# Expert rows added to the result in memory, in place of storing them and gathering them at the end

## The chip, the cores and the metric

The kernel runs on one core of one Trainium2 chip. The metric is the device time of one execution in microseconds (us), lower is better. The kernel before was timed in three runs: 1007.42, 1012.31 and 1018.16 us, median 1012.31.

## What is computed

The input x has 2048 rows (tokens) of 1024 numbers in float32, in eight sequences of 256. The reference does three things, here in its own words with what doesn't matter left out:

```python
y = einsum('bsi,boi->bso', x, cond_weight[itok])            # one of 8 matrices per sequence
gu = y @ shared_w_gate_up.T;  g, u = split(gu, 2)
shared = (silu(g) * u) @ shared_w_down.T                    # for every token
probs = softmax(y @ gate_w.T);  vals, idx = top_k(probs, 2) # 2 of 16 experts per token
combine = one_hot(idx) * (vals / sum(vals))
out_e = (silu(g_e) * u_e) @ w_down[e].T                     # inner width 256 per expert
out = x + shared + sum_e combine[:, e] * out_e
```

So each row of the result is the sum of four rows: x, the shared expert, and two chosen experts, the last two scaled by their weights.

## The kernel before, in words

Matrix products are made in float32 precision out of three products of a high and a low part. Every weight tile is loaded by SP into a staging buffer "st" (four of them), ScalarE writes its high part and VectorE its low part into "hl" (the function split, L83 to L86), and TensorE multiplies. load_w (L114) does this, and after each load it takes one piece of other work from the list "between" and queues it on VectorE behind that split.

The stages follow one another:

1. cond(0) to cond(7) (L238) make y for the eight sequences and write it to the memory tensor y_d. The rows come back through POOL (y_block, L385, tile "yr") and are transposed. In between run the stages a to d of Up (L445), which make the shared expert's inner values for the first half of the tokens (groups 0 and 1 of 512 rows). Up needs sums of weights; they are made once (sums_weights, L507) and kept in the memory tensor ss_d.
2. For each group of 512 tokens, route (L287) picks two experts per token and gives each pair a place in its expert's list. scatter (L371) writes token number and weight to that place of the table tab_d, by eight indirect DMAs per group from POOL.
3. Behind the last group, VectorE sorts the experts by their number of tokens (L1046 to L1060), so that the n-th expert in order has at most CAPS[n] rows (304 down to 256); one indirect DMA reads the table (entries, L882). Further VectorE instructions (L1061, L1062, L1075 to L1086) work out, for each token, at which row of os_d its two expert results will stand (s1i, s2i).
4. shared_down (L614) makes the shared expert's output for groups 0 and 1, adds x, and stores the sum to xs_d.
5. The expert loop (L1108 to L1126) runs 16 times. expert_rows (L906) gathers the expert's tokens by eight to ten indirect DMAs on POOL (tiles "yg" and "yl"); expert_yt transposes and splits them; expert_up (L832) and expert_out (L921) multiply. expert_down (L844) leaves 128 rows, already scaled by their weights, in a tile "o"; expert_down_last (L860) leaves the rows above 256 in "ol". The tag "o" has three buffers. SP stores the tiles to os_d (L925, L928), at rows that the order of the experts fixes.
6. Up runs again for groups 2 and 3, without storing sums. Meanwhile combine (L778), on POOL, reads xs_d for group 0, adds the two expert rows of each token by two indirect DMAs per 128 tokens that accumulate in SBUF, and stores to out; then it does the same for group 2 with x as the base, and leaves the tiles in SBUF.
7. DownPair.run (L700) makes the shared output of groups 2 and 3 together. Ahead of it, combine runs for group 1 (with a store) and then for group 3. run adds its products to the tiles of groups 2 and 3 (add, L716 to L719) and stores them (L721 to L725). The buffers for groups 1 and 3 are those of the pool pd (L1167), which opens when X is no longer read.

A loop for experts that exceed their capacity (L1225 to L1230) stands at the end; with these inputs its body doesn't run.

The order in which each engine issues its instructions is fixed when the program is built: the framework's scheduler orders the instructions of each engine by their place in the program and by when a timeline of its own says they can start, and issue_after holds a piece of work behind a given instruction. Each engine, and each engine's DMA issuing, then runs its list in order, so an instruction that waits holds up what is behind it in the same list. Semaphore waits are put in from the reads and writes of tiles and memory tensors.

Of the kernel before, what the change touches and what calls it, by code (L numbers as in the profile page):

```python
# [8 lines left out]

F32 = mybir.dt.float32  # L10
FR = mybir.dt.float32r
BF = mybir.dt.bfloat16
I32 = mybir.dt.int32
# [20 lines left out]
ROW0 = [sum(CAPS[:n]) for n in range(E + 1)]  # L34
ZROW = ROW0[E]
PAD = 4 * T


@with_exitstack
def adapter_moe_kernel(ctx: ExitStack, tc: tile.TileContext, xT, x, itok, wc, gate, wgu, wd, sgu, sd, out):  # L40
# [20 lines left out]
    lpad.tile([P, 48], F32, tag="lpad", name="lpad")  # L61
# [6 lines left out]
    tab_d = dram.tile([E * SLOTS, 2], I32, tag="tab_d", name="tab_d")  # L68
    os_d = dram.tile([ZROW + 16, H], F32, tag="os_d", name="os_d")
    xs_d = dram.tile([T, H], F32, tag="xs_d", name="xs_d")  # L70
# [70 lines left out]
    gpk = cpool.tile([P, NC * 2 * E + P + 80], FR, tag="gpk", name="gpk")  # L141
# [13 lines left out]
    tid = [cpool.tile([P, T // P, 2], I32, tag=f"tid{r}", name=f"tid{r}") for r in range(2)]  # L155
    rev = cpool.tile([P, NB, E], F32, tag="rev", name="rev")
    caps = cpool.tile([P, E], F32, tag="caps", name="caps")
    row0 = cpool.tile([P, E], F32, tag="row0", name="row0")
    oneh = [cpool.tile([P, T // P, E], BF, tag=f"oneh{r}", name=f"oneh{r}") for r in range(2)]
    ranks = [cpool.tile([P, T // P], F32, tag=f"ranks{r}", name=f"ranks{r}") for r in range(2)]  # L160
    places = [cpool.tile([P, T // P], I32, tag=f"places{r}", name=f"places{r}") for r in range(2)]
    s1i = cpool.tile([P, T // P], I32, tag="s1i", name="s1i")
    s2i = cpool.tile([P, T // P], I32, tag="s2i", name="s2i")
# [4 lines left out]
    cw = cpool.tile([P, 3, E], F32, tag="cw", name="cw")  # L168
    ix = cpool.tile([P, E, 10], I32, tag="ix", name="ix")

    def constants(ring):
# [10 lines left out]
        rt = ring.tile([P, 1024], I32, tag="op", name="rt")  # L182
        revi = rt[:, : NB * E].rearrange("p (k e) -> p k e", k=NB)
# [4 lines left out]
        for j in range(E):  # L188
            nc.gpsimd.memset(row0[:, j : j + 1], float(ROW0[j] - ZROW))
# [5 lines left out]
    def tables(ring):  # L195
        gst = ring.tile([P, 1024], F32, tag="op", name="gst")
        gv = gst[:, : NC * E].rearrange("p (c e) -> p c e", c=NC)
        nc.sync.dma_start(gv, gate)
        gs = gpk[:, : NC * 2 * E].rearrange("p (c l e) -> p l c e", c=NC, l=2)
        split(gs[:, 0], gs[:, 1], gv)  # L200
        ti = ring.tile([P, 1024], I32, tag="op", name="ti")
        tw = ti[:, : 2 * E * SLOTS // P].rearrange("p (f o) -> p f o", o=2)
        nc.gpsimd.memset(tw[:, :, 0], PAD)
        nc.gpsimd.memset(tw[:, :, 1], 0)
        nc.sync.dma_start(tab_d.rearrange("(p f) o -> p f o", p=P), tw)


    def zeros(ys):
# [4 lines left out]
        nc.gpsimd.dma_start(os_d[ZROW : ZROW + 16, :], zr[:16, :])  # L213
# [73 lines left out]
    def route(g, lp):  # L287
# [71 lines left out]
        for r in range(2):  # L359
            rank = ranks[r][:, gs]  # L360
            sl = t2(f"sl{r}")
            v.tensor_copy(oneh[r][:, gs, :], oh[r])
# [8 lines left out]
    def scatter(g):  # L371
        for r in range(2):
# [11 lines left out]

    def y_block(tb, ys):  # L385
        r = ys.tile([P, 1024], F32, tag="yr", name="yr")

        nc.gpsimd.dma_start(r, y_d[tb].rearrange("a (i t) f -> (a i) (t f)", t=4))  # L388
# [15 lines left out]
    lps = {}  # L404

# [372 lines left out]
    def combine(pool, tbs, base):  # L778
        acc = [pool.tile([P, 1024], F32, tag="ca", name="ca") for tb in tbs]
        for a, tb in zip(acc, tbs):  # L780
            nc.gpsimd.dma_start(a, base[tb * P : (tb + 1) * P, :])
        for si in (s1i, s2i):
            for a, tb in zip(acc, tbs):
                nc.gpsimd.indirect_dma_start(
                    out=a,
                    out_offset=None,
                    in_=os_d[:, :],
                    in_offset=bass.IndirectOffsetOnAxis(ap=si[:, tb : tb + 1], axis=0),
                    compute_op=ALU.add,
                )  # L790
        return acc
# [90 lines left out]
    def entries(pool, column):  # L882
        cr = pool.tile([P, ENTRIES, 2], F32, tag="cr", name="cr", bufs=1)
# [10 lines left out]
        def weights():  # L894
            ct = psm.tile([P, 3, E], F32, tag="sm", name="ct")
            with tc.issue_after(last_product[0]):
                for j in range(3):
                    m = min(P, CAP - j * P)
                    nc.tensor.transpose(ct[:m, j, :], cr[:E, j * P : j * P + m, 1], ident[:E, :E])
            for j in range(3):  # L900
                m = min(P, CAP - j * P)
                nc.vector.tensor_copy(cw[:m, j, :], ct[:m, j, :])
# [18 lines left out]
    def expert_out(po, n, at):  # L921
        w = load_wd(expert_id(n))
        r0 = ROW0[n]
        for j in range(2):
            nc.sync.dma_start(os_d[r0 + j * P : r0 + (j + 1) * P, :], expert_down(po, at, w, j * P, cw[:, j, n : n + 1]))  # L925
        if CAPS[n] > MAIN:
            m = CAPS[n] - MAIN
            nc.sync.dma_start(os_d[r0 + MAIN : r0 + CAPS[n], :], expert_down_last(po, at3[n % 2], w, m, cw[:m, 2, n : n + 1]))  # L928
# [28 lines left out]
    between[:] = [None, after_loads(lambda: tables(ring))]  # L957
    cond(1, ys, early)
    between[:] = [turned(0, 0), None, both(turned(0, 1), fetch_rows(1, up.place(0, 1)))]
# [18 lines left out]
    scatter(0)  # L978
# [19 lines left out]
    scatter(1)  # L998
# [9 lines left out]
    fetch_rows(6, tv)()  # L1008
    h0, h1 = half_works(3, 0, tv), half_works(3, 1, tv)
    up.stage_c(0)  # L1010
    scatter(2)
    up.stage_c(1)
    between[:] = [turned(6, 0), None, turned(6, 1), None, h0[0], h0[1]]
    cond(7, ys)
    fetch_rows(7, tv)()
    up.stage_c(2)
    up.stage_c(3)
    between[:] = [turned(7, 0), turned(7, 1)]
    up.stage_d(0)
    between[:] = [h1[0], h1[1]]  # L1020
    up.stage_d(1)
# [239 lines left out]
```

## Time and profile before

| what | us |
|---|---|
| median of the three runs | 1012.31 |
| the profiled execution, its own time | 1013.59 |
| its span, first to last instruction | 1011.8 |
| TensorE (PE) busy | 980.6 |
| VectorE (DVE) busy | 684.5 |
| ScalarE (ACT) busy | 542.8 |
| POOL busy | 329.4 |
| the expert stage, roughly | 457 to 757 |

A second table gives the DMA issues that the change touches, as the profile lists them: how many, how large, and the median time from issue to landing.

| issue | queue | number | KB each | us to landing |
|---|---|---|---|---|
| os_d from o | SP | 32 | 512 | 3.9 |
| os_d from ol | SP | 11 | 32 to 192 | 4.1 to 5.7 |
| xs_d from acc | SP | 16 | 256 | 4.8 |
| ca from xs_d | POOL | 8 | 512 | 6.0 |
| ca from x | POOL | 8 | 512 | 6.3 |
| ca from os_d (s1i), accumulating | POOL | 16 | not listed | 9.3 |
| ca from os_d (s2i), accumulating | POOL | 16 | not listed | 13.4 |
| out from ca | POOL | 8 | 512 | 11.0 |
| yg from y_d, a quarter of a block | POOL | 128 | not listed | 5.3 |
| tab_d from tid | POOL | 32 | not listed | 5.1 |

How to read it: a name such as "ca<-os_d,s1i" means that the tile ca is written from the tensor os_d with the indices s1i. "L719" is a line of the kernel. PE is TensorE's matmuls; PEld its weight loads, which overlap them. Matmuls are pipelined, so the length of a single row (395 ns for a 512-wide one) isn't the rate; the rate is the time of a long unbroken stretch over its number of matmuls. A busy time of POOL for a DMA is the time to issue it. The DMA share is the mean busy share of the core's 16 DMA engines.

### The profile page before, as it was taken

The page shows a single profiled execution, that of the slowest core. Times are in us where ns is not written, and L with a number is a line of the kernel's source. Part 1 is how long each engine was busy: PE and PEld are TensorE (multiplying, and loading weights), DVE is VectorE, ACT ScalarE, POOL GpSimd, SP SyncE. Part 2 cuts the span into 40 slices and gives each one's busy share as a digit, 9 for nine tenths or more (in the row PEclk, how much of TensorE's full clock was granted, in tenths as well). Part 3 has the DMA queues.
Part 4 walks back from the last instruction along what each step waited for, and adds up shares of the span by engine and source line. Part 5 has one row for each costly group of instructions (what it writes and reads, how often), then busy time and mean ns, then how long its engine had stood idle before and what let it go on. Part 6 is the DMA issues. An engine that isn't in the chain of part 4 may idle for free.

```text
span 1011.8 us, 14020 instructions
## 1 busy us (share of the span) xinstructions
PE 980.6 (97%) x5004; PEld 835.8 (83%) x5004; DVE 684.5 (68%) x915; ACT 542.8 (54%) x729; POOL 329.4 (33%) x330
## 2 busy tenths in 40 slices
PE   8999999989999999999999999999999997999976
PEld 6888887768878888889999999999988886888855
DVE  4576878846855986639788788779693433678634
ACT  5555545645734642316677677677574644335430
POOL 2000250221040036607888856530004350003450
PEclk9999999999999999999999999999999998999998
DMA  8999968878678546858798887888878998425996
GB/s 274 315 320 360 336 191 294 322 205 293 174 206 266 208 91 203 279 176 276 250 320 297 307 291 276 291 301 287 287 259 275 284 325 230 123 86 158 270 269 180
DMA packets 84204, 256.93 MB, mean 254 GB/s; under 512 B 13084, under 2 KB 21420, under 8 KB 84124
## 3 DMA queue, kind: packets, MB, share of 16 engines
q1 hardware_dynamic: 51084, 176.58, 52.3%
q0 software_dynamic: 21904, 69.79, 23.2%
q10 hardware_dynamic: 11136, 9.57, 2.8%
q8 instruction: 41, 0.67, 0.3%
q14 instruction: 39, 0.32, 0.1%
HBM read 207.62 MB, written 48.28 MB: 253 GB/s over the span
## 4 chain that ended last, share of the span: by engine, by line
PE 67%; DMA 10%; DVE 3%; issue 2%; ACT 1%; POOL 0%; ACTq 0%; POOLq 0%; DVEq 0%
PE acc L497 23%; PE acc L134 13%; PE acc L136 13%; PE acc L135 13%; DMA ca<-os_d,s2i 2%; PE acc L867 2%; DMA st<-ss_d 2%; PE acc L691 2%; DMA raw<-sd 2%; DMA out<-ca 1%; DVE hl L85 1%; DMA ca<-os_d,s1i 1%; DVE op L85 1%; DMA st<-wc 1%; DMA y_d<-yrow 1%
## 5 line engine op out<-in xcount | busy, mean ns | idle before, releaser
L85 DVE TENSOR_TENSOR hl<-st,hl 128x1024 fp32r<-128x1024 f32 (+1 forms) x254 | 304.3, 1209 | 184.7 <-ACT hl L84 183.4
L84 ACT CAST hl<-st 128x1024 fp32r<-128x1024 f32 (+1 forms) x254 | 263.0, 1043 | 191.9 <-PE acc L136 96.9
L497 PE MATMUL acc<-op,hl 128*128 128x512 f32 x1296 | 304.3, 395 | 9.8 <-DVE op L85 5.6
L497 PEld LDWEIGHTS acc<-op,hl 128*128 128x128 f32 x1296 | 246.4, 191 | 62.7 <-DVE op L85 6.0
L799 POOL DMA_INDIRECT yg<-y_d,ix x128 | 172.9, 1351 | 95.2 <-DVE tt L218 47.6
L136 PE MATMUL acc<-yte,hl 128*128 128x256 f32 (+6 forms) x512 | 147.3, 288 | 0.0
L134 PE MATMUL acc<-yte,hl 128*128 128x256 f32 (+6 forms) x512 | 147.1, 288 | 0.0
L135 PE MATMUL acc<-yte,hl 128*128 128x256 f32 (+6 forms) x512 | 147.0, 287 | 0.0
L135 PE MATMUL acc<-hl 128*128 128x512 f32 x256 | 101.1, 395 | 1.2 <-DVE hl L85 1.1
L136 PE MATMUL acc<-hl 128*128 128x512 f32 x256 | 100.5, 392 | 0.0
L135 PEld LDWEIGHTS acc<-yte,hl 128*128 128x128 f32 x512 | 96.5, 188 | 0.6
L134 PEld LDWEIGHTS acc<-yte,hl 128*128 128x128 f32 x512 | 96.3, 188 | 0.6
L136 PEld LDWEIGHTS acc<-yte,hl 128*128 128x128 f32 x512 | 96.2, 188 | 0.0
L134 PE MATMUL acc<-hl 128*128 128x512 f32 x256 | 90.5, 392 | 3.2 <-ACT hl L84 3.2
L388 POOL DMA_DIRECT2D yr<-y_d x24 | 13.2, 550 | 224.4 <-DMA y_d<-yrow 107.5
L374 POOL DMA_INDIRECT tab_d<-tid,places x32 | 41.0, 1280 | 63.6 <-DVE ranks L364 46.3
L134 PEld LDWEIGHTS acc<-hl 128*128 128x128 f32 x256 | 48.0, 189 | 14.4 <-ACT hl L84 4.6
L135 PEld LDWEIGHTS acc<-hl 128*128 128x128 f32 x256 | 48.3, 189 | 13.3 <-DVE hl L85 3.1
L136 PEld LDWEIGHTS acc<-hl 128*128 128x128 f32 x256 | 48.5, 189 | 10.0
L691 PE MATMUL acc<-shl,op 128*128 128x512 f32 x192 | 45.8, 400 | 9.0 <-DVE ca L719 9.0
L691 PEld LDWEIGHTS acc<-shl,op 128*128 128x128 f32 x192 | 37.2, 194 | 17.3 <-DVE ca L719 9.4
L134 PE MATMUL acc<-hl,at 128*128 128x512 f32 x128 | 50.0, 391 | 0.0
(221 smaller groups left out, 1397.0 us busy)
## 6 DMA issues: line engine op xcount, KB each, us to landing
st<-wgu SPq DMA_DIRECT2D x64, 512.0 KB, 4.8
st<-wc SPq DMA_DIRECT2D x63, 512.0 KB, 6.0
st<-wd SPq DMA_DIRECT2D x32, 512.0 KB, 5.6
os_d<-o SPq DMA_DIRECT2D x32, 512.0 KB, 3.9
st<-ss_d SPq DMA_DIRECT2D x30, 512.0 KB, 8.1
st<-sd SPq DMA_DIRECT2D x30, 512.0 KB, 3.8
yr<-y_d POOLq DMA_DIRECT2D x24, 512.0 KB, 6.0
st<-sgu SPq DMA_DIRECT2D x24, 512.0 KB, 6.3
```

Source lines behind the costliest of these rows:

```text
L84: last_cast[0] = nc.scalar.copy(hi, src).ins
L85: last_split[0] = nc.vector.tensor_tensor(lo, src, hi.bitcast(F32), op=ALU.subtract).ins
L134: nc.tensor.matmul(ps, lhs[0], rhs[0], start=first, stop=False)
L135: nc.tensor.matmul(ps, lhs[0], rhs[1], start=False, stop=False)
L136: last_product[0] = nc.tensor.matmul(ps, lhs[1], rhs[0], start=False, stop=last).ins
L374: i = nc.gpsimd.indirect_dma_start(out=tab_d[:, :], out_offset=bass.IndirectOffsetOnAxis(ap=places[r][:, tb : tb + 1], axis=0), in_=tid[r] ...
L388: nc.gpsimd.dma_start(r, y_d[tb].rearrange("a (i t) f -> (a i) (t f)", t=4))
L497: last_product[0] = nc.tensor.matmul(ps, lhs[x], rhs[y], start=(first and c == 0 and i == 0), stop=(c == 3 and i == 2), skip_group_check=T ...
L691: nc.tensor.matmul(ps[k], lhs[x], rhs[y], start=(first and t == c == i == 0), stop=(t == c == 1 and i == 2), skip_group_check=True,)
L799: last_gather[0] = nc.gpsimd.indirect_dma_start(out=r[:, t * 256 : (t + 1) * 256], out_offset=None, in_=y_d.rearrange("k a p f -> (k a p) f"),
L867: nc.tensor.matmul(ps, a3[:, fi, :], w[fi][:, l, hs], start=(fi == 0 and l == 0), stop=(fi == 1 and l == 1))
```

## The change

- The result tensor out gets 320 more rows (ENTRIES) behind its 2048; they are cut off after the run. os_d, xs_d, the indices s1i and s2i, and the VectorE work for them are gone.
- A table entry has three numbers in place of two: the third is the token's row in out. Unused entries point at distinct spare rows. entries transposes two columns in place of one (six small transposes on TensorE in place of three) and leaves the row numbers in ctok.
- expert_out calls add_out for each of its two or three tiles: an indirect DMA from POOL that adds the rows to out in memory. The adds of one expert carry no dependency among themselves; each has a real wait for all adds of the expert before.
- shared_down writes to out in place of xs_d for groups 0 and 1. For groups 2 and 3, x_to_out copies x to out, 2 MB each, memory to memory, on SP behind stage d.
- combine is gone: groups 0 and 1 need nothing more, and for groups 2 and 3 added_rows loads out into SBUF, four plain loads of 512 KB each, behind all adds.
- The table's scatters of groups 0 and 1 move from stages a and b to behind cond(6), that of group 2 from stage c(0) to behind cond(7), that of group 3 from before to behind the last stage d, each behind the last y load; the filling of the table, and pieces of the "between" lists (row transposes, router products and choices, the weight sums t1 and t2 of DownPair) move to later loads.

```diff
-        for j in range(2):
-            nc.sync.dma_start(os_d[r0 + j * P : r0 + (j + 1) * P, :], expert_down(po, at, w, j * P, cw[:, j, n : n + 1]))
+        for j in range(2):
+            add_out(expert_down(po, at, w, j * P, cw[:, j, n : n + 1]), ctok[:, j, n : n + 1])
         if CAPS[n] > MAIN:
             m = CAPS[n] - MAIN
-            nc.sync.dma_start(os_d[r0 + MAIN : r0 + CAPS[n], :], expert_down_last(po, at3[n % 2], w, m, cw[:m, 2, n : n + 1]))
+            add_out(expert_down_last(po, at3[n % 2], w, m, cw[:m, 2, n : n + 1]), ctok[:m, 2, n : n + 1])
+        adds[:] = [adds[1], []]
...
+    adds = [[], []]
+
+    def add_out(o, tok):
+        i = nc.gpsimd.indirect_dma_start(
+            out=out, out_offset=bass.IndirectOffsetOnAxis(ap=tok, axis=0), in_=o, in_offset=None, compute_op=ALU.add
+        ).ins
+        for k in adds[0]:
+            tc.add_manual_dep(i, k.name, SYNC, reason="adds to the same rows")
+        for k in adds[1]:
+            tc.declare_no_dep(i, k, reason="different rows")
+        adds[1].append(i)
...
+    def x_to_out(k):
+        ts = slice(T // 2 + k * GT, T // 2 + (k + 1) * GT)
+        after_loads(lambda: nc.sync.dma_start(out[ts, :], x[ts, :]))()
...
     def scatter(g):
+        with tc.issue_after(last_rows[0]):
+            scatter_now(g)
...
-    between[:] = [None, after_loads(lambda: tables(ring))]
     cond(1, ys, early)
-    between[:] = [turned(0, 0), None, both(turned(0, 1), fetch_rows(1, up.place(0, 1)))]
+    between[:] = [turned(0, 0), None, both(turned(0, 1), fetch_rows(1, up.place(0, 1))), after_loads(lambda: tables(ring))]
...
     fetch_rows(6, tv)()
+    scatter(0)
+    scatter(1)
     h0, h1 = half_works(3, 0, tv), half_works(3, 1, tv)
     up.stage_c(0)
-    scatter(2)
     up.stage_c(1)
-    between[:] = [turned(6, 0), None, turned(6, 1), None, h0[0], h0[1]]
+    between[:] = [None, None, turned(6, 0), None, turned(6, 1), None, h0[0], h0[1]]
     cond(7, ys)
     fetch_rows(7, tv)()
+    scatter(2)
     up.stage_c(2)
     up.stage_c(3)
-    between[:] = [turned(7, 0), turned(7, 1)]
+    between[:] = [None, turned(7, 0)]
     up.stage_d(0)
-    between[:] = [h1[0], h1[1]]
+    x_to_out(0)
+    between[:] = [turned(7, 1), h1[0]]
     up.stage_d(1)
+    x_to_out(1)
+    between[:] = [h1[1]]
+    up.stage_d(2)
     between[:] = [choices(3)]
-    up.stage_d(2)
+    up.stage_d(3)
     scatter(3)
-    up.stage_d(3)
...
-    shared_down(0, G, ring, acc, xs_d)
+    shared_down(0, G, ring, acc, out)
...
-    combine_kept(pc, 0, xs_d)
...
-    store_kept()
-    acc2 = combine(pc[1], range(2 * NB, 3 * NB), x)
+    acc2 = added_rows(pc, 2)
     down = DownPair((G, S_), raw)
     up.stage_c(0)
     down.fetch()
-    for u in range(1, 4):
-        between[:] = down.work((down.t1, down.t2, lambda t: None)[u - 1])[:1]
-        up.stage_c(u)
-        held(down.work((down.t1, down.t2, lambda t: None)[u - 1])[1])
+    up.stage_c(1)
+    up.stage_c(2)
+    w1, w2 = down.work(down.t1), down.work(down.t2)
+    between[:] = w1[:1]
+    up.stage_c(3)
+    held(w1[1])
+    between[:] = [None, w2[0]]
     up.stage_d(0)
-    between[:] = [None] * 4 + down.work(down.s3)
+    between[:] = [None, w2[1], None, None] + down.work(down.s3)
...
     pd = pool("pd", 4)
-    combine_kept(pd, 1, xs_d)
-    store_kept()
-    acc3 = combine(pd[1], range(3 * NB, 4 * NB), x)
+    acc3 = added_rows(pd, 3)
     down.run(2, ring, (acc2, acc3), out)
```

## The prediction

> **What bounds the kernel now.** I read the page first, for the engine that is never idle.
>
> ```profile
> span 1011.8 us, 14020 instructions
> PE 980.6 (97%) x5004; PEld 835.8 (83%) x5004; DVE 684.5 (68%) x915; ACT 542.8 (54%) x729; POOL 329.4 (33%) x330
> PE   8999999989999999999999999999999997999976
> POOL 2000250221040036607888856530004350003450
> DMA  8999968878678546858798887888878998425996
> ```
>
> TensorE bounds nearly everything. Only the windows show where it falls short. Columns: window, us, busy time and instructions of each engine, clock, DMA share, GB/s.
>
> ```profile
> 470.00:550.00 80.00, 80.00 (x515) 74.90 (x515) 65.80 (x91) 58.94 (x95) 66.90 (x44) 1.00 0.86 290
> 832.00:853.00 21.00, 15.79 (x70) 12.76 (x68) 5.46 (x5) 11.73 (x16) 4.16 (x3) 0.99 0.97 262
> 853.00:890.00 37.00, 36.65 (x150) 30.09 (x151) 24.37 (x28) 9.49 (x10) 0.00 (x0) 0.92 0.40 122
> 970.00:990.00 20.00, 10.98 (x46) 8.81 (x45) 4.98 (x6) 3.06 (x3) 11.23 (x8) 0.80 1.04 210
> 978.00:987.00 9.00, 1.66 (x8) 1.04 (x6) 0.00 (x0) 0.00 (x0) 5.72 (x4) 0.73 1.06 200
> 990.00:1012.00 22.00, 15.75 (x62) 11.88 (x61) 8.75 (x14) 0.00 (x0) 0.00 (x0) 0.89 0.52 173
> ```
>
> There are two holes behind the experts. The DMA share is at or above 0.97 as each begins, and the clock is low after them. The timeline of TensorE and the chain of waits say what each waits for.
>
> ```profile
> 879.76 38.24 PE L497 MATMUL acc<-op,hl 128*128 128x512 f32 x168
> 988.68 5.61 PE L691 MATMUL acc<-shl,op 128*128 128x512 f32 x16 [9.02 <-DVE ca L719]
> ```
>
> ```profile
> 834.30 16.53 DMA raw<-sd
> ...
> 947.89 13.94 DMA out<-ca
> 961.83 0.28 issue
> 962.12 6.27 DMA ca<-x
> 968.39 0.26 issue
> 968.65 8.64 DMA ca<-os_d,s1i
> 977.30 0.26 issue
> 977.56 9.68 DMA ca<-os_d,s2i
> ```
>
> The undisturbed rate is 38.24 / 168 = 0.2276 us per 512-wide matmul. The last hole is the combine: the second half's buffers open only at 924, and base, two accumulating gathers, stores, then base and two gathers again follow one another until VectorE can add (L719) and give TensorE banks. The first hole is a weight load of 16.5 us beside the other combine; VectorE waits for it (L669).
>
> **What the Trainium skill says.** "DMA: Bandwidth & Descriptors", section Rules for kernel authors: an accumulate reads its destination and writes it later, so another access of the same bytes must wait for its semaphore. The trace agrees: the second gather starts at 977.56, after the first has landed. Same page, section Issuing engines are not separate DMA queues: SP, ACT and POOL share the same 16 engines, so moving stores from SP to POOL buys no bandwidth; no row here contradicts it. "Perfetto Trace Analysis", section DMA Instruction — SWDGE (GPSIMD): a POOL row ends when its descriptors are written, not when the data lands. The trace agrees: a combine gather is 1.54 us on POOL and lands after a median of 9.3. "SBUF — State Buffer", section Who interferes with whom: VectorE can hold up GpSimd's descriptor writing through shared ports. The expert gathers do stretch, from 0.95 to 5.18 us; no row names the cause.
>
> **The change, part by part.** The sum is made against the profiled execution, 1013.6 us (span 1011.8), 1.3 above the median of 1012.3.
>
> *The combine at the tail.* 970 to 1005.86 holds 46 + 62 = 108 matmuls, which at 0.2276 need 24.6 us; they took 35.9. Lost: 11.3 us. After the change acc3 needs only four plain loads of 512 KB behind 924 (like ca<-x, 6 us each, overlapping), ready by about 935, and its first use is behind 960. All 11.3 come back; next late is TensorE itself. Between 0 and -11.3; I take -11.
>
> *The combine at 768 to 850.* 832 to 890 holds 220 matmuls, 50.1 us in 58: 8 lost. Sixteen accumulating gathers, their bases and stores leave the DMA engines around this stage and the tail, and the weight sums (t1, t2) move one stage later, so VectorE no longer waits in front of a load. Between 0 and -8; I take -7.
>
> *The stores become adds.* 43 stores leave SP and 43 adds come onto POOL: 32 of 128 rows, 11 with 256 rows between them. SP then no longer holds weight loads behind a wait for ScalarE (40.2 us in all at L925); TensorE is full in this stage, so that gains nothing. Three resources pay.
>
> POOL: from 458.82 to 583.27, 71 gathers ran with no gap but 0.3 us each, 1.753 us apart. An add isn't in the trace; the nearest rows are the combine gathers, 1.54 us at least and 1.75 on the mean. Lower bound per add 1.84 with the gap, upper 2.6 (the longest row); I take 2.05. An expert with a third block then costs 9 x 1.753 + 3 x 2.05 = 21.9 us of POOL, where TensorE turns an expert over in 19.4. Before, POOL rested:
>
> ```profile
> 599.62 1.81 POOL L799 DMA_INDIRECT yg<-y_d,ix  x1 [0.30 <-issue]
> 606.59 0.95 POOL L799 DMA_INDIRECT yl<-y_d,ix  x1 [5.17 <-DVE tt L218]
> 664.39 0.95 POOL L799 DMA_INDIRECT yg<-y_d,ix  x1 [7.88 <-DVE tt L218]
> ```
>
> So POOL falls behind by 2.5 us per expert over 11 experts. What hides it: gathers run three to four experts ahead (those of expert 15 start at 664, while expert 11 is multiplied), so 50 us of lag is harmless if it is the gathers that lag. If the adds lag it is not: "o" has three buffers, an add must land before ScalarE writes the same buffer one expert later, and a third block is ready at 575.0 (expert 4) and its buffer wanted at 588.0. With 1.6 us of issue and some 5 to 7 us to land, slack is 5 to 6 us.
>
> DMA engines: hardware-queue transfers took 52.3% of 1011.8 us for 176.58 MB, 3.0 us per MB, 1.57 per 512 KB. In 978 to 987, nearly all accumulating gathers, 9 x 1.06 us moved 1.8 MB: 5.3 us per MB, 2.8 per block. The adds cost (2.8 - 1.57) x 34 blocks = 42 us more over 470 to 757, whose shares of 0.86, 0.85, 0.85 and 0.80 are 242 us; 284 of 287 would be used. It fits, barely, and full shares have left TensorE at full rate (757 to 832: share 0.98, 333 matmuls in 75 us, 0.225 each).
>
> The wait: the first add of an expert waits on POOL for all adds of the one before, with gathers queued behind it. The last was issued some 11 us earlier; I expect 0 to 2 us, inside the gathers' lead.
>
> Together, between -1 and +40 us; with adds ahead of gathers I take +3, for a few late weights.
>
> *The front.* Table scatters move behind later y loads, and the last table is ready about one stage (48 x 0.2276 = 10.9 us) later. First gathers then start near 396 instead of 384.8; the first expert's product starts near 457, so the cover holds; without it up to 10 us. The x copies (two of 2 MB, memory to memory) pass through SP's ring ahead of weight loads: at 3.0 us per MB 6 us each, beside a DMA share of 0.46 (350 to 390) and four weight buffers of 5.5 us each. Removed VectorE work (the index sums, about 8 us near 380 to 399) was under full TensorE. Three more transposes of 0.15 us: +0.5. TensorE idled 7.9 us in 150 to 300, of which a freer POOL may return 2. Between -4 and +10; I take -1 in all.
>
> Sum: 1013.6 - 11 - 7 + 3 - 1 = 997.6, near 997 against the median shown.
>
> **Rivals.** *Adds late in POOL's order* (30%). The order of a queue is fixed when the program is built; if it counts gathers as quicker than 1.75 us, adds stand behind gathers that POOL has not reached. By the end of expert 4 POOL has 67 gathers and 15 adds behind it, 458.8 + 117.5 + 30.8 = 607; the last add was ready at 575. Less the slack (6) and what TensorE has in hand (about 5), it loses some 20 at worst, half of that if gathers run at the 1.5 us of after 583. So +8 to +20 in place of +3: 1002 to 1016, likeliest 1008. For it: POOL without rest from 458 to 582 already. Against: an add comes earlier in the program than the gathers it competes with. A tail that gives back only one hole ends here too.
>
> *Adds dear in the DMA engines* (23%, slower). The known accumulates write to SBUF; these read and write memory rows. With c us per block the stage needs 242 + 34 (c - 1.57), and at the highest share seen, 1.05, there are 301. The 18 us gained are gone from c = 3.9. At 4.5 the stage takes 325 instead of 287, +38: 1033. For it: HBM carries the destination twice. Against: 809 to 820 moved 421 GB/s at share 1.03, so memory isn't the limit at 290.
>
> *The changed kernel runs as meant* (47%): 990 to 1003, likeliest 997.
>
> **How the numbers follow.** 1% is about what these runs (1007 to 1018) tell from no change. The first case lies on the faster side but for 1 in 100, the second in the middle but for 2 on either side, the third on the slower: 0.48, 0.27, 0.25. The range 988 to 1020 leaves out most of the third case and little else.
>
> **What would show it.** Right: no TensorE gap before L719 behind 970 and none for raw<-sd; shares of 0.95 to 1.0 in the experts; landing of adds below 10 us; expert period still 19.4. The first rival shows as ScalarE waiting for an add before "o" or "ol" with POOL busy throughout and periods near 21; the second as landings of 15 us and more with TensorE waiting for st. A TensorE gap at the table's transposes would make my front term wrong.

## The result, and the profile after

The changed kernel takes 1070.05 us (median of 4 runs, 1067.57 to 1073.65), the kernel before 1012.67 in the runs beside it: a ratio of 1.057, 95% interval 1.050 to 1.063. It is slower by some 57 us, where the forecast was 997 us with a range of 988 to 1020.

The profiled execution took 1068.68 us with a span of 1066.9. The page, with the same rows as shown of before:

```profile
span 1066.9 us, 13949 instructions
PE 1000.8 (94%) x5007; PEld 847.7 (79%) x5007; DVE 677.3 (63%) x891; ACT 541.5 (51%) x729; POOL 349.6 (33%) x313
PE   8999999999999989999988888798989599999997
POOL 2000201010434158178877777776222100000000
DMA  8899969686796557687678878778988733533322
```

TensorE now has 8s and a 7 in slices 21 to 26, where POOL has its 7s and 8s (19 to 27), and a 5 in slice 32. The last seven slices are better than before. The windows (columns: window, us, busy time and instructions of PE, PEld, DVE, ACT and POOL, clock, DMA share, GB/s) show the experts, first in the kernel before and then in the changed one, and the changed kernel from 839.69 us to its last product:

```profile
550.00:600.00 50.00, 50.00 (x345) 47.43 (x345) 38.67 (x51) 35.35 (x55) 37.55 (x30) 1.00 0.87 292
600.00:650.00 50.00, 50.00 (x329) 46.17 (x328) 40.91 (x53) 37.56 (x59) 27.27 (x22) 1.00 0.83 285
```

```profile
550.00:600.00 50.00, 44.30 (x256) 39.15 (x256) 30.25 (x41) 28.63 (x46) 37.37 (x25) 0.90 0.80 223
600.00:650.00 50.00, 41.42 (x256) 36.75 (x256) 30.03 (x41) 28.36 (x46) 37.38 (x25) 0.96 0.78 220
839.69:1061.00 221.31, 221.31 (x966) 182.74 (x966) 125.59 (x132) 99.45 (x132) 4.16 (x8) 0.99 0.38 124
```

In the experts there are 256 matmuls in 50 us, where the kernel before had 345 and 329, and the DMA engines are *less* busy than before. The last row is the second half behind its first 42 products: TensorE is full throughout, so neither of the two holes of the kernel before is left. (The experts end some 60 us later now, so the same work stands that much later on the clock.)

To see where the time went I cut the span at three marks that both kernels have: the first product of a third block, the rows of an expert above 256, which experts 0 to 10 have (expert 0, L867 before and L873 after), the last of them (expert 10), and the first product of the second half's Up (L497 before, L506 after).

| piece of the span, us | before | after | difference |
|---|---|---|---|
| start to the first third-block product | 488.4 | 485.6 | -2.8 |
| experts 0 to 10 ("the stretch") | 195.1 | 242.1 | +47.0 |
| experts 11 to 15, to the second half's first product ("the end of the experts") | 73.5 | 90.6 | +17.1 |
| the second half | 254.8 | 248.6 | -6.2 |
| span | 1011.8 | 1066.9 | +55.1 |

An expert of the stretch takes 24.2 us in place of 19.5. Three lines of the view of waits of the changed kernel within the stretch (who waits, for whom; us, times, longest) name ScalarE (ACT) waiting for adds to land, and GpSimd (POOL) waiting too:

```profile
ACT ol L874 <- DMA out<-ol,ctok: 41.9, 9, 5.9
ACT o L862 <- DMA out<-o,ctok: 30.9, 9, 7.4
POOL out L790 <- ACT ol L874: 23.4, 8, 3.8
```

And this is one expert of GpSimd's timeline (start, duration, what, in brackets the idle time before it), six of the eight gathers in the middle left out:

```profile
568.35 1.40 POOL L790 DMA_INDIRECT out<-ol,ctok  x1 [0.30 <-issue]
572.76 1.59 POOL L790 DMA_INDIRECT out<-o,ctok  x1 [3.02 <-ACT ol L874]
574.66 4.71 POOL L805 DMA_INDIRECT yl<-y_d,ix  x1 [0.30 <-DVE tt L218]
579.67 1.75 POOL L790 DMA_INDIRECT out<-o,ctok  x1 [0.30 <-ACT s L831]
581.73 1.01 POOL L805 DMA_INDIRECT yg<-y_d,ix  x1 [0.30 <-issue]
...
592.02 0.94 POOL L805 DMA_INDIRECT yg<-y_d,ix  x1 [0.30 <-issue]
593.26 1.39 POOL L790 DMA_INDIRECT out<-ol,ctok  x1 [0.30 <-issue]
597.56 1.59 POOL L790 DMA_INDIRECT out<-o,ctok  x1 [2.90 <-ACT ol L874]
```

The add of a third block (out<-ol) stands in the order behind eight gathers for an expert six places later. Once it is issued, the next expert's first add has to wait until it has landed, since both may touch the same rows; that wait is 2.9 us on the mean and 3.8 at most. The view puts it down to ScalarE's copy into ol, but that copy waits for the same landing (the first line above); run B2 below takes away only the wait of one expert's adds for those of the expert before, and GpSimd's gap is gone. In between there is no gap but 0.30. So GpSimd is either issuing or waiting for a landing, for 24.9 us in this expert, and TensorE follows it.

The piece behind the stretch shows a second thing. TensorE stops once more at the second half's first stage:

```profile
818.34 9.68 PE L506 MATMUL acc<-op,hl 128*128 128x512 f32 x42
839.69 2.93 PE L506 MATMUL acc<-op,hl 128*128 128x512 f32 x6 [11.66 <-ACT X L543]
```

```profile
827.00 1.53 POOL out L790
828.53 0.30 issue
828.84 10.11 DMA out<-o,ctok
839.05 0.59 ACT X L543
```

The second fence is the chain of waits: the tile X lies where source tiles of adds had been, so ScalarE's first copy into it (L543) waits until the last expert's last add has landed.

### The profile page after: what moved, and what is told of

Read it like the earlier page. It is cut to its first block, busy times and chain, and to the rows that moved or that the text cites. A ratio compares the mean times of both kernels' runs of the same rounds, so it can differ in the third digit from the quotient of the medians.

```text
span 1066.9 us, 13949 instructions
## 1 busy us (share of the span) xinstructions
PE 1000.8 (94%) x5007; PEld 847.7 (79%) x5007; DVE 677.3 (63%) x891; ACT 541.5 (51%) x729; POOL 349.6 (33%) x313
## 5 line engine op out<-in xcount | busy, mean ns | idle before, releaser
L506 PE MATMUL acc<-op,hl 128*128 128x512 f32 x1296 | 300.5, 392 | 11.8 <-ACT X L543 11.7
L506 PEld LDWEIGHTS acc<-op,hl 128*128 128x128 f32 x1296 | 243.9, 189 | 63.6 <-ACT X L543 12.3
L805 POOL DMA_INDIRECT yg<-y_d,ix x128 | 160.8, 1256 | 69.2 <-issue 40.3
L133 PE MATMUL acc<-yte,hl 128*128 128x256 f32 (+6 forms) x512 | 150.8, 296 | 14.9 <-DVE s L832 7.6
L135 PE MATMUL acc<-yte,hl 128*128 128x256 f32 (+6 forms) x512 | 149.9, 293 | 0.0
L134 PE MATMUL acc<-yte,hl 128*128 128x256 f32 (+6 forms) x512 | 149.7, 293 | 0.0
L133 PEld LDWEIGHTS acc<-yte,hl 128*128 128x128 f32 x512 | 99.1, 194 | 18.0 <-DVE s L832 9.4
L134 PEld LDWEIGHTS acc<-yte,hl 128*128 128x128 f32 x512 | 99.2, 194 | 0.4
L135 PEld LDWEIGHTS acc<-yte,hl 128*128 128x128 f32 x512 | 99.0, 194 | 0.0
L790 POOL DMA_INDIRECT out<-o,ctok x32 | 61.4, 1918 | 67.7 <-ACT ol L874 27.8
L134 PE MATMUL acc<-hl,at 128*128 128x512 f32 x128 | 56.2, 439 | 14.5 <-DVE hl L84 14.5
L133 PE MATMUL acc<-hl,at 128*128 128x512 f32 x128 | 55.2, 431 | 10.5 <-ACT hl L83 9.0
L862 ACT ACTIVATE o<-acc,cw 128x512 f32<-128x512 f32 x64 | 40.5, 684 | 38.5 <-DMA out<-o,ctok 37.9
```

The costliest lines, as they stand in the source:

```text
L133: nc.tensor.matmul(ps, lhs[0], rhs[0], start=first, stop=False)
L134: nc.tensor.matmul(ps, lhs[0], rhs[1], start=False, stop=False)
L135: last_product[0] = nc.tensor.matmul(ps, lhs[1], rhs[0], start=False, stop=last).ins
L506: last_product[0] = nc.tensor.matmul(ps, lhs[x], rhs[y], start=(first and c == 0 and i == 0), stop=(c == 3 and i == 2), skip_group_check=T ...
L790: i = nc.gpsimd.indirect_dma_start(out=out, out_offset=bass.IndirectOffsetOnAxis(ap=tok, axis=0), in_=o, in_offset=None, compute_op=ALU.ad ...
L805: last_gather[0] = nc.gpsimd.indirect_dma_start(out=r[:, t * 256 : (t + 1) * 256], out_offset=None, in_=y_d.rearrange("k a p f -> (k a p) f"),
```

## Experiments

Each run is one edit to a kernel, or several that are named, with its cut into the same four pieces. Two kernels with nearly the same order of GpSimd gave 210.4 and 222.4 us for the stretch, so less than some 12 us between two stretches decides nothing here. The kernel before took 1004 to 1034 us beside these runs, which were made on several chips (1014 to 1034 on one of them alone). Where no median is given, a whole time is that of one execution. So the argument rests on the pieces, compared with those of the profile above, and not on the whole times. The expectations count the end of the experts to the 43rd product of the second half, behind X's wait (112 us in the changed kernel); the table counts to the first (90.6).

| run | start | stretch | end of the experts | second half | whole |
|---|---|---|---|---|---|
| changed kernel | 485.6 | 242.1 | 90.6 | 248.6 | 1068.7 |
| A1 gathers of m behind adds of m-6 | 482.4 | 217.7 | 94.7 | 249.4 | 1046.4 |
| A2 behind adds of m-5 | 486.1 | 210.4 | 93.7 | 248.7 | 1040.7 |
| A3 behind adds of m-4 | 493.7 | 225.6 | 91.8 | 246.7 | 1059.6 |
| B1 plain scatters | 483.2 | 224.9 | 90.8 | 241.3 | 1042.0 |
| B2 two targets | 504.1 | 222.4 | 96.5 | 244.2 | 1069.0 |
| C before, no gathers of the combination | 486.6 | 195.1 | 79.7 | 235.3 | 998.9 |
| D1 rows loaded by SyncE | 485.2 | 236.0 | 84.5 | 244.6 | 1052.1 |
| D2 = A3 + D1 | 484.4 | 229.9 | 95.3 | 245.9 | 1057.3 (median 1047.0) |
| D3 = A2 + D1, X moved | 484.5 | 222.4 | 88.0 | 234.5 | 1031.2 |
| D4 = D3, finer order | 485.9 | 219.9 | 86.7 | 234.6 | 1028.4 |
| E1 = A1, half the bytes per add | 485.6 | 220.6 | 89.5 | 245.7 | 1041.0 |
| E2 = D4, half the bytes per add | 479.2 | 219.2 | 82.9 | 234.5 | 1018.0 |
| F1 = A1 without subtractions | 485.5 | 195.1 | 79.3 | 245.5 | 1007.2 |
| F2 = D4 without subtractions | 484.9 | 195.1 | 73.2 | 234.5 | 989.6 |

### A. Is it the order of the adds in GpSimd's queue?

My first theory after the result was my own first rival, larger than I had made it: adds stand behind gathers made too early. The edit fixes how far gathers may run ahead of adds (n - 4 puts the gathers of expert m = n + 2 behind the last add of m-6):

```diff
     adds = [[], []]
+    last_add = []
...
+        last_add.append(adds[1][-1])
         adds[:] = [adds[1], []]
...
         if n + 2 < E:
-            rs = expert_rows(pa[1], n + 2)
+            with tc.issue_after(last_add[n - 4] if n >= 4 else last_gather[0].ins):
+                rs = expert_rows(pa[1], n + 2)
```

> The changed kernel with one edit of order: the gathers of expert m stand on POOL behind the last add of expert m - 6, so that no third-block add waits behind eight gathers. The same instructions, bytes and waits. Order theory: the first to the last third-block product on TensorE takes 242 us in the changed kernel and 195 before; it falls to 200 to 212, and the time from 1070 to 1025 to 1040. If the adds are dear in the DMA engines, the order changes nothing: 235 us or more, 1062 or more.

Measured: 217.7 us for the stretch and 1046.4 in all, between the two theories. 24 of the 47 us went, so the order is a cause; more was left than expected. The timeline of A1 says why: GpSimd now has no wait at all, and is still slower than TensorE.

```profile
607.01 1.64 POOL L791 DMA_INDIRECT out<-o,ctok  x1 [0.30 <-DMA yg<-y_d,ix]
608.95 3.80 POOL L806 DMA_INDIRECT yl<-y_d,ix  x1 [0.31 <-issue]
613.05 1.78 POOL L791 DMA_INDIRECT out<-o,ctok  x1 [0.30 <-ACT at L83]
615.14 1.41 POOL L791 DMA_INDIRECT out<-ol,ctok  x1 [0.30 <-issue]
616.86 1.03 POOL L806 DMA_INDIRECT yg<-y_d,ix  x1 [0.31 <-issue]
...
626.71 0.94 POOL L806 DMA_INDIRECT yg<-y_d,ix  x1 [0.30 <-issue]
627.96 4.98 POOL L791 DMA_INDIRECT out<-o,ctok  x1 [0.31 <-issue]
```

From 607.01 to 627.96 is 21 us for twelve instructions. If that is the bound, gathers that run less far ahead should give time back once for each expert of lead that is spent. The same edit with n - 3 and n - 2:

> The changed kernel, but the gathers of expert m are put into GpSimd's order behind the last add of expert m-5, one expert later than in the run before (m-6). Theory of GpSimd's capacity (nine gathers and three adds take it about 21.7 us per expert against TensorE's 19.5, and an order that always asks for gathers five or six experts ahead keeps that excess on the path): one expert less of lead frees nine gathers, 12 to 15 us, once, so the stretch from the first to the last third-block product (experts 0 to 10) takes 203 to 208 us instead of 217.7 and the whole 1030 to 1040. Rival, the adds' landing alone holds ScalarE at the o tiles whatever the order: the stretch stays at 215 to 220 and the whole at 1043 to 1050.

Measured 210.4 and 1040.7: only 7 us better than A1, which is within the scatter, and between the two theories.

> The same with the gathers of expert m behind the last add of expert m-4. Theory of capacity: the stretch comes to 195 to 202 us, near the 195.1 of the kernel before, since TensorE is then the bound as long as the lead lasts; what follows it to the second half's first Up stage stays at 110 to 125 us (the eight loads of rows stand on GpSimd behind the last gathers, which come later still), so the whole takes 1022 to 1038. Rival, the landing alone: 215 to 220 and 1043 to 1050.

Measured 225.6 and 1059.6: wrong for both theories. The view of waits shows a new one in the place of the old: with every gather behind the third block's add, GpSimd stands idle until that product exists, and rows come late.

```profile
DVE tt L218 <- DMA yg<-y_d,ix: 57.4, 11, 7.0
POOL out L791 <- ACT ol L877: 46.2, 10, 6.1
```

Here VectorE (L218) waits 57 us for the gathers into yg; in the changed kernel's stretch it doesn't wait for those at all, and 13.3 us for the ones into yl. One queue holds two streams with different deadlines, and no order of it that I tried meets both.

### B. Is it the addition, or the landing between experts?

B1 leaves the addition out (each scatter overwrites), with the waits between experts kept:

```diff
-            out=out, ..., in_=o, in_offset=None, compute_op=ALU.add
+            out=out, ..., in_=o, in_offset=None
```

> The changed kernel with plain scatters in place of adding ones: the addition is left out, the rows overwrite those of out. POOL's order and all waits stay. Order theory: POOL's loop per expert shrinks only by what an issue gets shorter (1.6 to 1.9 us before, perhaps 1.0 now) and by a quicker landing, so 215 to 235 us for the third-block stretch and 1042 to 1063 in all. If the accumulation in the DMA engines is the cause, the stretch falls to 195 to 200 and the time to 1000 to 1020.

Measured: stretch 224.9, whole 1042.0, the first within the order theory's range and the second at its edge. A scatter that only writes also costs GpSimd less (1.41 us on the mean for 128 rows, 1.93 with the addition). It saves 17 of the 47 us and leaves 30; the dear accumulation in the DMA engines (my second rival) would have left next to nothing.

B2 adds the experts with odd numbers to a second tensor, which is zeroed first and not brought into the result, so that an expert waits for the one two before it:

```diff
-            out=out, ..., compute_op=ALU.add
+            out=(out, odd_d)[n % 2], ..., compute_op=ALU.add
```

> The changed kernel with the odd experts' rows added to a second memory tensor, so that an expert's first add waits for the expert before the last one; the second tensor isn't merged, the odd experts' rows are left out of the result. Order theory: the 3 us that POOL stands per expert until the third-block add has landed go, the rest of its loop stays: the third-block stretch 210 to 225 us in place of 242, 1035 to 1055 in all. If the wait between experts is the whole cause: 195 to 200 and 1000 to 1020. If the adds are dear in the DMA engines: nothing, 1062 or more.

Measured: stretch 222.4, as expected; the whole, 1069.0, was not: the edit also zeroes another 2368 rows of 4 KB, TensorE has a gap of 16 us behind that, and the first mark comes 18.5 us later. GpSimd's order is that of the changed kernel, the wait between experts is gone, and GpSimd is busy 41.5 to 41.8 us of every 50 with 28 or 29 instructions, which with 28 gaps of 0.30 is all of it:

```profile
600.00:650.00 50.00, 46.44 (x299) 42.96 (x300) 34.97 (x48) 33.44 (x54) 41.76 (x28) 0.97 0.91 261
```

So A1 and B2 take away the landing wait in two ways and end at the same place, near 220.

### C. What are the removed gathers worth alone?

The kernel before, without the eight accumulating gathers of each of its four combinations, so that the experts' rows are missing from its result:

```diff
-        for si in (s1i, s2i):
-            for a, tb in zip(acc, tbs):
-                nc.gpsimd.indirect_dma_start(
-                    out=a, ..., compute_op=ALU.add)
```

> The kernel before with the 32 accumulating gathers of the combine left out, so the experts' rows are left out of the result; bases are still loaded and groups 0 and 1 still stored. It measures what the tail can give. By the working of the prediction (18 us of full-rate time lost behind 832): 992 to 997. If the combine also slowed what looked full: 980 to 990. If something else holds the tail: above 1003.

Measured 998.9 in all, and a second half of 235.3 in place of 254.8: 19.5 us, for 18 in my sum (11 and 7). The stretch is 195.1, as before. The whole misses the expected 992 to 997 by 2 us, as the end of the experts came out 6 us longer.

### D. The end of the experts, and everything together

D1 issues the second half's eight loads of rows (yr) from SyncE (SP); on GpSimd they stood behind the last gathers and between adds.

```diff
-    def y_block(tb, ys):
+    def y_block(tb, ys, q=None):
...
-        last_rows[0] = nc.gpsimd.dma_start(r, ...).ins
+        last_rows[0] = (q or nc.gpsimd).dma_start(r, ...).ins
...
-                for work in batch_rows((self.g0 + n) * 2 + k, self.ys, self.place(n, k)):
+                for work in batch_rows((self.g0 + n) * 2 + k, self.ys, self.place(n, k), nc.sync):
```

> The changed kernel with one edit: the eight loads of rows for the second half's Up are issued by SyncE instead of GpSimd. Theory that these loads, queued on GpSimd behind gathers and between adds, make the 38 us between the last third-block product and the second half's first Up stage: that piece takes 80 to 95 us instead of 112 and the whole 1050 to 1060; the stretch before it stays at 238 to 245. Rival, it is the adds of the last experts and their landing that hold this piece: it stays at 105 to 115 and the whole at 1065 to 1073.

Measured 1052.1; the piece by the expectation's count is 102.6, between the two theories. Of the 9 us saved, 6 are in the table's piece and 3 behind it. The loads were a part and not the whole.

> Both edits: gathers of expert m behind the last add of expert m-4, and the second half's eight loads of rows on SyncE. If the two causes are the whole loss and add up: the stretch of experts 0 to 10 195 to 202 us, the piece after it 75 to 92, the whole 990 to 1012, within 2% of the kernel before and most likely faster. If GpSimd's capacity is still on the path, the loss comes out again at the last experts: the piece after it stays over 100 and the whole over 1015.

Measured 1047.0 (median of 5; ratio to before 1.028, 1.020 to 1.036), far from the 990 to 1012 of two separate causes. The profiled execution took 10 us more than the other four, so its stretch of 229.9 may be high; it shows no gain of the order m-4.

D3 goes back to m-5, and gives yr its place in the pool pb ahead of the adds' source tiles, so that X no longer lies on any of these:

```diff
+    pb[1].tile([P, 1024], F32, tag="yr", name="yr")
     at = expert_up(pb[1], 0, yt)
```

> Three edits to the changed kernel: gathers of expert m behind the last add of expert m-5 (as in the run that gave 210.4 us for the stretch of experts 0 to 10), the second half's eight loads of rows on SyncE (which took 9.3 us off the piece after it), and the tile X of the second half's Up laid where no add's source tile was (it waited 12 us for the last experts' adds to land). If these are separate causes: stretch 207 to 214, piece after it 115 - 9 - 11 = 92 to 98 us, whole 1015 to 1025. If X's wait only hid another (the last experts' products themselves late), the piece stays at 103 to 110 and the whole at 1026 to 1034.

Measured: the second half takes 234.5 us in place of 248.6 and the piece by the expectation's count 97.5, which was expected if X's wait was a cause of its own. It was, and with it gone the second half is 20.3 us shorter than before the change. The whole, 1031.2, misses since the stretch came out at 222.4.

D4 lets the first four gathers stand behind the second add of expert m-5 and only the rest behind its last:

```diff
-        last_add.append(adds[1][-1])
+        last_add.append([adds[1][1], adds[1][-1], adds[1][-1]])
...
+        for j, (t0, k, m) in enumerate(blocks):
+            with tc.issue_after(behind[j]) if behind else nullcontext():
+                rs.append((gather_rows(pg, ix[:, n, :], t0, k), k, m))
```

> The same, and GpSimd's order within an expert is finer: the first four gathers stand behind the second add of expert m-5, and only the other four behind its third (or last) one, so that the wait of that add for its product (1 to 3 us per expert) is filled with gathers. If GpSimd's idle waits are what remains in the stretch of experts 0 to 10: 200 to 207 us instead of 210, whole 1005 to 1018, within 1% of the kernel before. If the DMA engines (share 0.86 to 0.91 in the run with m-5) or the gathers' issue itself hold it: stretch 208 to 214 and whole 1015 to 1025.

Measured: stretch 219.9, 1028.4 in all (4 runs; ratio 1.020, interval 1.017 to 1.024). GpSimd's idle waits fall from 14.5 us in the stretch (D3) to 3.5, and the stretch has hardly moved; it is worse than both theories said. This is the best version with the whole computation in it, and it is still slower than the kernel before.

### E. GpSimd's issue, or the adds' bytes?

Both would fit a stretch near 220. Here each add moves 512 of its 1024 columns, as many rows and instructions for half the bytes:

```diff
-            out=out, ..., in_=o, in_offset=None, compute_op=ALU.add
+            out=out.rearrange("r (h f) -> (r h) f", h=2), ...,
+            in_=o[:, :512], in_offset=None, compute_op=ALU.add
```

> Leaves out half of the addition: each add moves only the first 512 of the 1024 columns of its rows, and to half rows elsewhere in the result, so it is as many instructions with as many rows on GpSimd for half the bytes in the DMA engines. Gathers of expert m behind the last add of expert m-6, where GpSimd had no gap but 0.30 us and the stretch of experts 0 to 10 took 217.7 us. If GpSimd's issue of nine gathers and three adds per expert is the bound there: the stretch stays at 210 to 220 us and the whole at 1032 to 1046. If it is the adds' bytes and their landing (ScalarE waited 46 us for o tiles): 196 to 206 us and the whole 1015 to 1030.

> The same half of the addition left out of the best ordered kernel so far (m-5 with the finer order, the loads of rows on SyncE, X off the adds' tiles; stretch of experts 0 to 10 219.9 us, 1028.4 us). If GpSimd's issue holds what is left of the loss there: stretch 212 to 222, whole 1018 to 1028. If the adds' bytes and landing do: stretch 196 to 207, whole 1000 to 1014.

Measured: 220.6 and 219.2 us for the stretch (217.7 and 219.9 with all bytes), while the DMA share in it fell to 0.68 to 0.81. An add of 128 rows landed sooner too (a median of 6.3 us in E1, 8.9 in the changed kernel). So bytes and landing aren't the bound. GpSimd's issue is: in the stretch of A1, E1 and E2 it has no gap but 0.30. E2's whole, 1018.0, is 10 us lower, from the pieces around the stretch.

### F. Why does GpSimd need 21.8 us?

The shortest rows seen are 0.94 us for a gather and 1.55 for an add of 128 rows, with 0.30 between rows: 9 x 1.24 and 3 x 1.85 make 16.7 us per expert, less than TensorE's 19.5. The rows are longer than that, irregularly: 4.71, 3.80, 4.98 above. In the trace of the kernel before, the experts' gathers with no VectorE instruction beside them took 0.955 us (13 rows), those beside one of the split's subtractions (L85) 1.43 on the mean (111 rows). That alone proves little, since a long row is also more likely to meet a subtraction. So the last two runs leave out the subtractions for the experts' weights, six of 1.2 us per expert; TensorE multiplies the high halves in their place (whole[0] is False in the expert loop alone):

```diff
-        end = split(hl[:, 0, :], hl[:, 1, :], st)
+        if whole[0]:
+            end = split(hl[:, 0, :], hl[:, 1, :], st)
+        else:
+            end = nc.scalar.copy(hl[:, 0, :], st).ins
+            hl = hl[:, 0:1, :].to_broadcast([P, 2, 1024])
```

> Leaves out VectorE's subtractions for the low halves of the experts' weights (one of 128x1024 per weight load; TensorE multiplies the high halves in their place, as many matmuls as before). Otherwise gathers of expert m behind the last add of expert m-6, where nine gathers and three adds took GpSimd 21.8 us per expert. Theory that gathers' and adds' rows on GpSimd are stretched by VectorE's subtractions running beside them: the gathers' mean falls from 1.2 to 1.5 us to 0.95 to 1.1, the twelve take some 17 to 18.5 us per expert, and the stretch of experts 0 to 10 195 to 203 us instead of 217.7. Rival, the rows are stretched by the queue or the DMA engines (rings full): the mean stays at 1.2 and more and the stretch at 212 to 220.

> The same subtractions left out of the best ordered kernel (m-5 with the finer order, the loads of rows on SyncE, X off the adds' tiles; stretch 219.9 us, 1028.4 us). By VectorE's theory: gathers' mean 0.95 to 1.1, stretch 194 to 200, whole 998 to 1008. By the rival: stretch 212 to 222, whole 1018 to 1030.

Measured: the stretch is 195.1 us in both, the very number of the kernel before, with TensorE full. TensorE is full there in the kernel before too, so that kernel has nothing to gain in the stretch from the same omission. The groups of GpSimd's rows within the stretch (xcount, busy us, mean ns; idle before), first A1 and then F1, the same but for the subtractions:

```profile
L806 POOL DMA_INDIRECT yg<-y_d,ix x88 | 103.8, 1180 | 26.8 <-issue 26.2 <-DMA st<-wgu 0.3 <-DMA yg<-y_d,ix 0.3
L791 POOL DMA_INDIRECT out<-o,ctok x20 | 50.9, 2544 | 6.1 <-issue 4.0 <-ACT at L83 0.9 <-ACT ol L875 0.3
L791 POOL DMA_INDIRECT out<-ol,ctok x10 | 15.0, 1498 | 3.0 <-issue 3.0
L806 POOL DMA_INDIRECT yl<-y_d,ix x7 | 13.7, 1961 | 2.1 <-issue 1.2 <-DVE at L84 0.6 <-DVE s L833 0.3
```

```profile
L811 POOL DMA_INDIRECT yg<-y_d,ix x88 | 89.5, 1017 | 30.7 <-issue 24.7 <-DMA out<-o,ctok 5.1 <-DMA yg<-y_d,ix 0.9
L796 POOL DMA_INDIRECT out<-o,ctok x21 | 33.9, 1614 | 9.7 <-ACT o L868 5.1 <-issue 2.1 <-ACT hl L122 0.9
L796 POOL DMA_INDIRECT out<-ol,ctok x10 | 13.7, 1373 | 8.9 <-ACT ol L882 7.1 <-issue 0.9 <-ACT at L83 0.3
L811 POOL DMA_INDIRECT yl<-y_d,ix x7 | 6.9, 987 | 2.1 <-issue 1.2 <-DVE yte L84 0.6 <-DVE tt L223 0.3
```

A1: 183.4 us of rows and 38.0 of gaps, as much as the stretch has (rows at its two ends are counted whole). F1: 144.0 of rows and, at 0.30 each, 37.8 of gaps, 182 of 195. The rows lost 39 us, the gathers came down to 1.02 us and the adds to 1.61, and GpSimd fits again, with 17 us in which it waits. In F2 even the end of the experts is back at 73.2 us. TensorE's granted clock over the stretch goes the same way (0.94 in the changed kernel, 0.98 in A1, 1.00 in F1 and in the kernel before), so a part of the loss shows as a lower clock and not as a gap. F1's windows show one thing more: TensorE at its full rate with the DMA engines as full as my sum had said.

```profile
550.00:600.00 50.00, 50.00 (x339) 47.04 (x338) 18.05 (x32) 33.67 (x53) 37.36 (x34) 1.00 0.99 283
600.00:650.00 50.00, 50.00 (x337) 46.57 (x336) 23.11 (x37) 39.52 (x61) 33.64 (x30) 1.00 0.96 287
```

F1 and F2 leave out VectorE's work too, not only its effect on GpSimd. VectorE was busy 30 of 50 us in the changed kernel, so it wasn't the bound. Shorter rows were needed in any case: in A1 GpSimd works without a gap but 0.30, so twelve rows cannot come round faster than every 21.8 us unless the rows shrink. Whether shorter waits for VectorE were needed as well isn't split further. That GpSimd's rows shrink when the subtractions go is shown; by which means the two engines meet isn't. The Trainium skill, "SBUF — State Buffer", section Who interferes with whom, says that a VectorE instruction with two inputs in SBUF contends with a GpSimd instruction that reads SBUF, and adds an inference that descriptor writing is spared by tensor_tensor. The subtraction is a tensor_tensor with two inputs in SBUF, an indirect DMA's offsets lie in SBUF, and the rows here did stretch; for these indirect DMAs the measurement speaks against the inference.

## Why the prediction was wrong

**The tail combine (-11) and the one at 768 to 850 (-7): right.** Together -18. The gathers alone were worth -19.5 in the second half (C), and the change gives -20.3 there once X doesn't wait (D3). In the changed kernel TensorE has no gap from 839.69 to its last product, neither for the weight load raw<-sd nor for the adds into ca (L728; L719 before), as the forecast asked. But only 6.2 us of the gain are left there, since 11.7 go to X.

**The front (-1): right**, -2.8.

**The stores become adds (+3): the step that failed.** Its working had the number: "An expert with a third block then costs 9 x 1.753 + 3 x 2.05 = 21.9 us of POOL, where TensorE turns an expert over in 19.4", and A1 measured 21.8. The agreement is in part luck: with the gap a gather took 1.54 us in A1's stretch, not 1.753, and an add 2.50, not 2.05. The error is in what follows, that the lag "is harmless if it is the gathers that lag". It isn't the gathers that lag. The fixed order keeps them six experts ahead throughout, and puts the adds behind them; so the whole excess, 10 x 2.3 = 23 us over the stretch, falls on the adds, whose buffers ScalarE wants an expert later. Allowing less lead (A2, A3) did not turn it into a lag of gathers that costs nothing: at m-4 the rows come late.

**The wait (0 to 2 us, "inside the gathers' lead"): wrong.** It is 2.9 us on the mean (3.8 at most) per expert, with GpSimd idle, because the third block's add is issued just before it and not 11 us earlier. It goes with the other 24 us of the stretch (A1), and B2, with the order unchanged, gives back 20 by dropping this wait alone. As GpSimd is the bound, each of those microseconds counts.

**The DMA engines (284 of 287 us used, "it fits, barely"): right**, though the changed kernel doesn't show it. Its shares of 0.73 to 0.80 between 500 and 700 us are those of engines that wait for orders; F1 has 0.96 to 0.99 with TensorE full. Over the stretch F1's share is 0.96, for 0.86 before.

**The end of the experts: not in my sum at all.** +17.1 us. Part is the same excess of GpSimd for five more experts; part is the eight loads of rows that GpSimd issues behind the last gathers (6 us by D1, and 6 between F1 and F2, though these differ in order too). X's 11.7 us come behind it, which is more than half of what the second half had gained.

**The rivals.** "Adds late in POOL's order" was the mechanism, down to its signs (ScalarE waiting for an add before o or ol, GpSimd busy). I gave it +8 to +20 because I took the lag at the end of expert 4 for the worst; GpSimd never catches up in the stretch, and the bill is 47 us in the stretch and most of 17 behind it. (By the forecast's own sum +20 makes 1014.6, not 1016.) "Adds dear in the DMA engines" is out by B1, E1 and E2. Of the 47, some 24 are order and landing (242.1 to 217.7) and some 23 go with the subtractions (217.7 to 195.1), both with the scatter of 12. The subtractions were left out in two better orders only, not in the changed kernel's own.

Open: why A2 and D3, with nearly the same order of GpSimd, differ by 12 us in the stretch (GpSimd's rows there add up to 160.7 us in A2 and 175.0 in D3, for 117 and 118 of them, so they stretched more in D3; why isn't known); and whether the subtractions could be written so that they leave GpSimd alone, which would be the way to a version faster than the kernel before. I didn't find such a version.

## What to carry to other kernels

When a change puts work on an engine that issues in order, multiply its rows out against the period of the bounding engine, and where the sum is larger take it as a new bound: a lead of earlier instructions on the same queue didn't hide it here, since in the fixed order it was the newcomers with the nearer deadline that stood behind. Before moving transfers to GpSimd, look at which VectorE instructions run beside its indirect DMAs: the shortest row says what it could take, the mean what it will. And look at what reuses the memory of the sources, since an add that lands late holds the next stage's tiles too.

## What the runs showed of the hardware

- Indirect DMAs issued by GpSimd take it longer when VectorE's subtractions with both inputs in SBUF run beside them: gathers into yg a mean of 1.18 us with them (A1) and 1.02 without (F1), adds of 128 rows 2.54 and 1.61. Single rows reached 5.5 us in A1's stretch and 8.6 in D2's; in F1's none was longer than 2.0. I had seen stretched rows before the forecast, and had not asked what they would be without.
- An accumulating scatter of 128 rows costs GpSimd 1.55 us at least, a plain one 0.98 (B1), a gather 0.94; with half the bytes in its rows the accumulating scatter still took 1.56 at least (E1).
- With the subtractions gone, DMA shares of 0.96 to 0.99 over 180 us (F1, 500 to 680) didn't hold TensorE back: it was busy in all of them.
